# A decoder layer's first stage: a quarter of the value weighing on GpSimd, and context projections in token halves, one position at a time

## The chip, the cores and the metric

The kernel runs on one core of a Trainium2 chip. The metric is the device time of one execution in microseconds (us), the median of several runs. A core has a matrix engine (TensorE, PE in the profile), a vector engine (VectorE, DVE), an activation engine (ScalarE, ACT), GpSimd (POOL) and SyncE (SP), which here only issues DMA transfers. Each runs its own queue of instructions in order and waits on semaphores for the others. SBUF and PSUM are the memories on the chip, with 128 partitions each; TensorE writes its results to PSUM.

## The reference, cut to what matters

One post-norm decoder layer in float32 on `x` of 8 positions x 512 batch entries x 512 features, with a context of 8 x 512 tokens x 1024 features:

```python
q, k, v = split(x @ in_proj.T + bias)            # 16 heads of 32, sequence of 8
ac = einsum('tbhd,sbhd->bhts', q + r_w_bias, k)
bd = rel_shift(einsum('tbhd,rhd->bhtr', q + r_r_bias, p))
attn = softmax((ac + bd) * scale)
ctx = einsum('bhts,sbhd->tbhd', attn, v)
x = layernorm(x + ctx @ out_proj.T + b)
src = (context @ W_src.T + b_src) * mask         # 1024 -> keys 512, values 512
x = layernorm(x + cross_attention(x, src))       # 8 heads of 64, 512 tokens
x = layernorm(x + ffn(x))                        # 2048 hidden, second product in fp8
```

## The kernel before

The first stage does the self-attention and the first normalization; between those it projects the context to the keys and values that the second stage (cross-attention and feed-forward, the rest of the span) attends to.

**Self-attention.** Partitions are batch entries, four tiles j of 128. `keys`, `queries_of` and `values` project 128 x 512 tiles on TensorE through `project` (L225); keys and values go to `k_all`, `v_all` by ACT (L295 for values), queries to DVE (L254). The attention over eight positions is elementwise. For one query position t, `queries_of` forms on DVE, for two groups of eight heads, the product of the query with all keys (L258, 2048 elements a partition) and sums it over the head (L267). After eight positions `softmax` runs on the tile's scores `sc`: GpSimd adds offsets (L301), DVE subtracts the maximum and divides, ACT takes the exponential (L308). Then `weigh(j, t)` (L317 to L340) does, per position, for two groups of eight heads: a product of `v_all` with the broadcast weights (L322, 2048 elements), and three additions that halve the key positions (L332, L335, L338: 1024, 512 and 256 elements), the last into `ao`. `turn_out` transposes `ao` on TensorE (L346) two positions later, `put_out` projects it (L355), and the sum with `x` and the output bias (GpSimd, L365; DVE, L372), its statistics and normalization follow. `ao` has two buffers, `sc`, `k_all` and `v_all` have one.

**Context projections.** Seven products of block sums replace eight products of blocks (Winograd's form of Strassen's scheme). `halves(part)` loads the four blocks of the weight (keys are part 0, values part 1) and sums them (L141 to L144); `context_of(m, part)` loads the context of two positions, 2m and 2m + 1, as columns of one product, sums its blocks on DVE (`sums_of_b`, L148 to L151), and stores the sums to HBM (`td`), from where part 1 loads them again. `context_work` is a generator: for each part, for m = 0, 1, 2, for two halves i of the output rows, it issues seven products `py`, `pz`, `px`, `pz`, ... of four matmuls with 512 columns (L697), moves results by ACT (`put`, L727) and DVE (`add`, L739) to `kst` tiles, and stores them to `kd` or `vd` on ACT's queue. In between, `sum_w1` has GpSimd form sums of another weight, `w1`, for the second stage. Positions 0 to 5 are done so; position 6 is done with plain products of blocks (`project_context`, L171 for keys, L185 for values) at the end of the stage, position 7 in the second stage.

**The order of TensorE's work** is written out by a planner (L384 to L449, L810 to L875), with `manual_schedule` for PE; the other engines' instructions are ordered by the tile framework's scheduler. Each slot has a planned length: `SCORES` for a position of the scores, `SOFTMAX`, and `VALUES` for a position of the weighing. In a slot the planner places what must be there, then `spare` projections, and fills up with pieces of `context_work`. Each piece yields its cost (`FULL` = 3.54), `"between"` (something else must come first) or a negative number (rest for so long). SP's queue carries nearly all loads, the planner's order being that in which they are issued.

Of the kernel before, what the change touches and what calls it, by code (L numbers as in the profile page):

```python
# [42 lines left out]
def decoder_layer(  # L43
# [156 lines left out]
    with ExitStack() as ph:  # L200
# [116 lines left out]
        def weigh(j, t):  # L317
            ao[t] = qp.tile([P, E], F32, tag="ao", name=f"ao{j}_{t}")
            for g in range(2):
                fs = slice(g * HW, (g + 1) * HW)  # L320
                pr = prp.tile([P, T, HH, D1], F32, tag="pr", name=f"pv{j}_{t}_{g}")
                nc.vector.tensor_tensor(  # L322
                    pr,
                    v_all[j][:, :, fs].rearrange("p s (h d) -> p s h d", d=D1),
                    sc[j][:, t, g * HH * T : (g + 1) * HH * T]
                    .rearrange("p (h s) -> p s h", s=T)
                    .unsqueeze(3)
                    .to_broadcast([P, T, HH, D1]),
# [3 lines left out]
                nc.vector.tensor_tensor(  # L332
                    pf[:, 0:4, :], pf[:, 0:4, :], pf[:, 4:8, :], ALU.add
                )
                nc.vector.tensor_tensor(  # L335
                    pf[:, 0:2, :], pf[:, 0:2, :], pf[:, 2:4, :], ALU.add
                )
                nc.vector.tensor_tensor(  # L338
                    ao[t][:, fs], pf[:, 0, :], pf[:, 1, :], ALU.add
                )  # L340
# [43 lines left out]
        SCORES, SOFTMAX, VALUES, FULL = 11.2, 13.0, 12.4, 3.54  # L384
# [73 lines left out]
        with tc.tile_pool(name="setup", bufs=1) as sp:  # L458
# [140 lines left out]
        cxp = ph.enter_context(tc.tile_pool(name="cxp", bufs=8))  # L599
        tcp = ph.enter_context(tc.tile_pool(name="tcp", bufs=4))  # L600
        kst = ph.enter_context(tc.tile_pool(name="kst", bufs=4))
# [6 lines left out]
        PAIRS = 3  # L608
        td = [
            [dram.tile([P, 5, S], F32, name=f"td{m}_{f}") for f in range(HF)]  # L610
            for m in range(PAIRS)
        ]
# [12 lines left out]
        def context_of(m, part):  # L625
            lo, hi, tx = [], [], []
            for f in range(HF):
                a = cxp.tile([P, 2, S], F32, tag="ct", name=f"cl{part}{m}_{f}")
                b = cxp.tile([P, 2, S], F32, tag="ct", name=f"ch{part}{m}_{f}")
                x = tcp.tile([P, 3, S], F32, tag="tx", name=f"tx{part}{m}_{f}")  # L630

                def two(f):
                    return ctxT[2 * m : 2 * m + 2, f * P : (f + 1) * P, :].rearrange(
                        "t p s -> p t s"
                    )

                nc.sync.dma_start(b, two(HF + f))
                if part == 0:
                    nc.sync.dma_start(a, two(f))
                    with tc.high_priority():  # L640
                        sums_of_b(
                            nc.vector,
                            *(u[:, h] for u in (a, b) for h in (0, 1)),
                            *(x[:, i] for i in range(3)),
                        )
                    nc.sync.dma_start(td[m][f][:, 0:2], a)
                    nc.sync.dma_start(td[m][f][:, 2:5], x)
                else:
                    nc.sync.dma_start(a, td[m][f][:, 0:2])
                    nc.sync.dma_start(x, td[m][f][:, 2:5])  # L650
                lo.append(a)
                hi.append(b)
                tx.append(x)
            return lo, hi, tx
# [23 lines left out]
        def context_work():  # L678
            for part in range(2):
                store_w1()  # L680
                w7 = halves(part)
                blocks = [(4 * part + n, f) for n in range(4) for f in range(2)]
                if part:

                    yield -12.0
                for m in range(PAIRS):
                    lo, hi, tx = context_of(m, part)
                    b11, t3 = [u[:, 0] for u in lo], [u[:, 1] for u in lo]
                    b21, b22 = [u[:, 0] for u in hi], [u[:, 1] for u in hi]
                    t1, t2, t4 = ([u[:, i] for u in tx] for i in range(3))  # L690
                    for i in range(2):

                        def product(bank, a, b, start):


                            for f in range(HF):
                                nc.tensor.matmul(  # L697
                                    bank,
                                    lhsT=w7[:, a, f, i * P : (i + 1) * P],
                                    rhs=b[f],  # L700
                                    start=start and f == 0,
                                    stop=f == HF - 1,
                                    skip_group_check=not start,
                                )

                        def bank(name):
                            return ps_kv.tile(
                                [P, S], F32, tag="kv", name=f"{name}{part}{m}_{i}"
                            )

                        st = {}

                        def order(u, names):
                            if part == 0:
                                return u
                            return u.rearrange(f"p ({names}) -> p s g e", g=4, e=32)

# [15 lines left out]
                        def add(r, c, src):  # L736
                            dst = order(st[r, c], "g s e")
                            with tc.high_priority():
                                nc.vector.tensor_tensor(dst, order(src, "s g e"), dst, ALU.add)  # L739
# [43 lines left out]

        w6, ct6 = ([], []), []
# [1081 lines left out]
```

## Time and profile before

| | us |
|---|---|
| median of 3 runs (1992.72 to 1994.48) | 1994.43 |
| profiled execution | 1994.99 |
| its span, first to last instruction | 1993.2 |
| PE busy in the span | 1964.2 |
| DVE busy | 1580.8 |
| ACT busy | 563.9 |
| POOL busy | 246.7 |
| mean granted TensorE clock | 0.996 |
| first query projection of the second stage starts | 864.26 |

A group of the profile names line, engine, operation, output <- inputs by tile names, shape and count; then busy time in us and the mean of one in ns; then the engine's idle time just before them and what ended it. A float32 matmul stands as two rows, so counts of PE are twice the matmuls. The ends of matmuls are modelled; their distance from start to start is the surer measure. In a timeline, a line is a start, a length and a run of like instructions.

### The profile page before, as it was taken

To read this page: it belongs to the slowest core of one execution; us is meant where nothing else is said; L and a number is where in the kernel's file an instruction comes from. 1 tells how busy PE (TensorE), PEld (TensorE's weight loads), DVE (VectorE), ACT (ScalarE), POOL (GpSimd) and SP (SyncE) were. 2 spreads that over 40 slices of the span, in tenths; PEclk is the share of its full clock that TensorE was granted. 3 is DMA by queue.
4 is the path that set the end of the run, shared out by engine and by line. 5 is a ranking of instruction groups with operands and counts; after the bars stand their busy time and mean duration, and the time that the engine had idled before them with its cause. 6 is when DMAs were issued, how large, how long until landed. Compare 5 with 4: busy or idle time off the path is not lost.

```text
span 1993.2 us, 20470 instructions
## 1 busy us (share of the span) xinstructions
PE 1964.2 (99%) x6936; PEld 1108.3 (56%) x6936; DVE 1580.8 (79%) x2485; ACT 563.9 (28%) x1226; POOL 246.7 (12%) x264
## 2 busy tenths in 40 slices
PE   9999999998999999999999999999999999999998
PEld 4544444444444444443457657567576565676776
DVE  4999999899899989656885886877958868678443
ACT  2111111120111011123235244253352542535322
POOL 0030022002301121113401001002010010000000
PEclk9999999999999999999999999999999999999999
DMA  6635136252342361578698767775877767765721
GB/s 228 227 116 220 39 114 230 75 210 62 107 174 71 108 220 61 159 262 222 169 211 248 163 168 219 154 216 159 197 201 167 174 207 164 226 154 141 202 92 61
DMA packets 247080, 328.87 MB, mean 165 GB/s; under 512 B 85312, under 2 KB 140608, under 8 KB 242752
## 3 DMA queue, kind: packets, MB, share of 16 engines
q1 hardware_dynamic: 229200, 291.09, 52.0%
q10 hardware_dynamic: 14496, 25.47, 3.5%
q0 software_dynamic: 3280, 11.01, 1.8%
q8 instruction: 55, 0.90, 0.2%
q14 instruction: 49, 0.40, 0.1%
HBM read 195.90 MB, written 64.49 MB: 131 GB/s over the span
## 4 chain that ended last, share of the span: by engine, by line
PE 76%; DVE 19%; issue 2%; ACT 1%; DMA 1%; POOL 0%; SPq 0%; DVEq 0%; ACTq 0%
PE hx L1388 11%; PE s L1114 6%; PE pox L1306 6%; PE hz L1388 5%; PE av L1215 5%; PE psq L1093 5%; PE o L1480 5%; PE px L697 5%; DVE sc L267 4%; PE po L355 4%; DVE pq L258 4%; PE psk L171 3%; PE psv L185 3%; PE ps_q L225 3%; PE hy L1388 3%; PE poz L1306 3%
## 5 line engine op out<-in xcount | busy, mean ns | idle before, releaser
L1139 ACT ACTIVATE pe<-pe,nmax 128x512 f32<-128x512 f32 x256 | 182.8, 715 | 178.9 <-DVE nmax L1129 178.4
L1129 DVE CUSTOM_DVE_ANT_0 pe<-s,mb 128x512 f32<-128x512 f32 x256 | 162.8, 682 | 29.1 <-PE s L1114 25.4
L1162 DVE STREAM_TRANSPOSE pb<-pe 128x512 f32<-128x512 f32 x256 | 162.2, 681 | 5.4 <-DMA raw<-vd 2.8
L258 DVE TENSOR_TENSOR pq<-qw,k 128x2048 f32<-128x2048 f32 x64 | 152.5, 2383 | 1.2
L322 DVE TENSOR_TENSOR pv<-v,sc 128x2048 f32<-128x2048 f32 x64 | 146.9, 2295 | 6.5 <-ACT v L295 4.8
L267 DVE TENSOR_REDUCE sc<-pq 128x64 f32<-128x2048 f32 x64 | 145.9, 2280 | 1.0
L1114 PE MATMUL s<-kT,qTx 64*128 64x512 f32 x512 | 127.5, 616 | 0.5 <-DVE nmax L1129 0.5
L225 PE MATMUL ps_q<-w_in,xt 128*128 128x512 f32 x256 | 117.8, 604 | 5.2 <-DVE qw L254 5.2
L1215 PE MATMUL av<-pT,vx 128*64 128x512 f32 x512 | 118.6, 606 | 2.8 <-DMA raw<-vd 2.8
L1388 PE MATMUL hx<-x2s,w1r 128*128 128x256 f32 x512 | 119.5, 384 | 0.8 <-DVE hs L1416 0.8
L225 PE MATMUL ps_k<-w_in,xt 128*128 128x512 f32 x256 | 115.0, 601 | 4.5 <-DMA xt<-in_xT_dram 4.5
L1388 PE MATMUL hx<-x2T,w1r 128*128 128x256 f32 x512 | 118.4, 381 | 0.6 <-ACT hs L1410 0.6
L1154 DVE TENSOR_SCALAR pe<-pe,rden 128x512 f32<-128x512 f32 x256 | 115.3, 493 | 4.6
L355 PE MATMUL po<-w_o,aoT 128*128 128x512 f32 x256 | 115.3, 593 | 0.9 <-ACT aoT L371 0.9
L225 PE MATMUL ps_v<-w_in,xt 128*128 128x512 f32 x256 | 114.4, 593 | 0.1
L1480 PE MATMUL o<-w2q,hq 128*128 128x512 fp8e4 x512 | 114.4, 379 | 0.0
L1093 PE MATMUL psq<-x1Ts,w_tgt 128*128 128x512 f32 x256 | 113.8, 597 | 0.6 <-PE av L1215 0.6
L1388 PEld LDWEIGHTS hx<-x2s,w1r 128*128 128x128 f32 x512 | 95.5, 190 | 28.8 <-DVE nmax L1129 13.7
L1388 PEld LDWEIGHTS hx<-x2T,w1r 128*128 128x128 f32 x512 | 96.5, 190 | 20.5 <-issue 6.9
L1417 ACT ACTIVATE hq<-hs 128x512 fp8e4<-128x512 f32 x96 | 60.5, 630 | 144.7 <-DVE hs L1416 144.7
L697 PE MATMUL px<-tx,w 128*128 128x512 f32 x192 | 88.4, 604 | 3.6 <-DVE st L739 3.4
L365 POOL TENSOR_TENSOR r<-r,bo 128x512 f32<-128x512 f32 x32 | 48.9, 1545 | 330.0 <-DMA r<-in_x_dram 230.5
(204 smaller groups left out, 3066.0 us busy)
## 6 DMA issues: line engine op xcount, KB each, us to landing
pT<-pb SPq DMA_DIRECT2D x480, 128.0 KB, 2.4
w1r<-w1d SPq DMA_DIRECT2D x32, 1024.0 KB, 7.1
w1r<-w1d SPq DMA_DIRECT2D x32, 768.0 KB, 5.8
ch<-in_ctxT_dram SPq DMA_DIRECT2D x24, 512.0 KB, 5.7
td<-tx SPq DMA_DIRECT2D x12, 768.0 KB, 4.9
tx<-td SPq DMA_DIRECT2D x12, 768.0 KB, 7.5
r<-in_x_dram SPq DMA_DIRECT2D x32, 256.0 KB, 3.5
x1Ts<-x1d SPq DMA_DIRECT2D x32, 256.0 KB, 6.4
```

The lines of the kernel that those rows point to most:

```text
L225: nc.tensor.matmul(ps, lhsT=xt[:, e, :], rhs=w_in[:, e, part * E : (part + 1) * E], start=(e == 0), stop=(e == EC - 1),)
L258: nc.vector.tensor_tensor(pr, qw[:, fs] .rearrange("p (h d) -> p h d", d=D1) .unsqueeze(2) .to_broadcast([P, HH, T, D1]), k_all[j][:, :, f ...
L267: nc.vector.tensor_reduce(sc[j][:, t, g * HH * T : (g + 1) * HH * T], pr.rearrange("p h s d -> p (h s) d"), AX.X, ALU.add,)
L355: nc.tensor.matmul(po, lhsT=aoT[t][:, c * P : (c + 1) * P], rhs=w_o[:, c, :], start=(c == 0), stop=(c == EC - 1),)
L697: nc.tensor.matmul(bank, lhsT=w7[:, a, f, i * P : (i + 1) * P], rhs=b[f], start=start and f == 0, stop=f == HF - 1, skip_group_check=not s ...
L1093: nc.tensor.matmul(ps, lhsT=w_tgt[:, e, o * P : (o + 1) * P], rhs=x1T[t][:, e, :], start=(e == 0), stop=(e == EC - 1),)
L1114: nc.tensor.matmul(ps[:, h, :], lhsT=qT[t, c][half[h], j * P : (j + 1) * P], rhs=kT[t, c][half[h], :], start=True, stop=True,)
L1139: nc.scalar.activation(pe, pe, AF.Exp, bias=nmax[:, h : h + 1], scale=-1.0, accum_out=den[:, h : h + 1],)
L1215: nc.tensor.matmul(av[half[h], :], lhsT=v[t, c][:, s, half[h]], rhs=pT[t, c][:, :, :, s, h].rearrange("p g i q -> p (g i) q"), start=(s == 0),
L1306: nc.tensor.matmul(xo_bank[name][:, i], lhsT=b[:, e, i * P : (i + 1) * P], rhs=w[:, e], start=start and e + i == 0, stop=e == EC - 1, skip ...
L1388: nc.tensor.matmul(banks[g, name][:, i], lhsT=w[:, f, i * P : (i + 1) * P], rhs=b[:, f], start=start and f + i == 0, stop=f == 1, skip_gro ...
L1480: nc.tensor.matmul(po, lhsT=rows_of_j, rhs=w2q[:, c, :], start=(c == 0), stop=(c == HC - 1),)
```

## The change

In `weigh`, GpSimd takes heads 12 to 15 (with a buffer pool `pgp` of its own) and DVE heads 0 to 5 and 6 to 11, with the same four operations each, all writing parts of one `ao`. `SCORES` goes from 11.2 to 12.0, `VALUES` from 12.4 to 11.6.

The context projections take one position at a time: the columns of a product are one half of the position's 512 tokens, so a product is eight matmuls of 256 columns (four blocks of features, two halves h of the output rows, both in one PSUM bank) and not four of 512. Keys of positions 0 to 6 and values of positions 0 to 5 are done so; the plain keys of position 6 go. The blocks of a position (four raw, three sums, 512 KB each) are tiles of one pool of 13 (`cxp`), asked for in the order of use up to 13 products ahead. The rests of 13, 3 and 6 between positions are removed; that of 12 between the parts stays. Results of two row halves go to one `st` tile and are stored together.

The diff, cut to its core (the new `ask_blocks` and the new body of `context_work` in full, the lines that they replace being those of `context_of` and `context_work` above):

```diff
             ao[t] = qp.tile([P, E], F32, tag="ao", name=f"ao{j}_{t}")
-            for g in range(2):
-                fs = slice(g * HW, (g + 1) * HW)
-                pr = prp.tile([P, T, HH, D1], F32, tag="pr", name=f"pv{j}_{t}_{g}")
-                nc.vector.tensor_tensor(
+            for eng, lo, hi in (
+                (nc.gpsimd, 12, H1),
+                (nc.vector, 0, 6),
+                (nc.vector, 6, 12),
+            ):
+                hs = hi - lo
+                fs = slice(lo * D1, hi * D1)
+                pr = (pgp if eng is nc.gpsimd else prp).tile(
+                    [P, T, hs, D1], F32, tag="pr", name=f"pv{j}_{t}_{lo}"
+                )
+                eng.tensor_tensor(
                     pr,
                     v_all[j][:, :, fs].rearrange("p s (h d) -> p s h d", d=D1),
-                    sc[j][:, t, g * HH * T : (g + 1) * HH * T]
+                    sc[j][:, t, lo * T : hi * T]
                     .rearrange("p (h s) -> p s h", s=T)
                     .unsqueeze(3)
-                    .to_broadcast([P, T, HH, D1]),
+                    .to_broadcast([P, T, hs, D1]),
                     ALU.mult,
                 )
                 pf = pr.rearrange("p s h d -> p s (h d)")
-                nc.vector.tensor_tensor(
+                eng.tensor_tensor(
                     pf[:, 0:4, :], pf[:, 0:4, :], pf[:, 4:8, :], ALU.add
                 )
-                nc.vector.tensor_tensor(
+                eng.tensor_tensor(
                     pf[:, 0:2, :], pf[:, 0:2, :], pf[:, 2:4, :], ALU.add
                 )
-                nc.vector.tensor_tensor(
-                    ao[t][:, fs], pf[:, 0, :], pf[:, 1, :], ALU.add
-                )
+                eng.tensor_tensor(ao[t][:, fs], pf[:, 0, :], pf[:, 1, :], ALU.add)
...
-        SCORES, SOFTMAX, VALUES, FULL = 11.2, 13.0, 12.4, 3.54
+        SCORES, SOFTMAX, VALUES, FULL = 12.0, 13.0, 11.6, 3.54
...
-        cxp = ph.enter_context(tc.tile_pool(name="cxp", bufs=8))
-        tcp = ph.enter_context(tc.tile_pool(name="tcp", bufs=4))
-        kst = ph.enter_context(tc.tile_pool(name="kst", bufs=4))
+        BLOCKS = 13
+        pgp = ph.enter_context(tc.tile_pool(name="pgp", bufs=1))
+        cxp = ph.enter_context(tc.tile_pool(name="cxp", bufs=BLOCKS))
+        kst = ph.enter_context(tc.tile_pool(name="kst", bufs=2))
         HF, W2 = FC // 2, E // 2
-        PAIRS = 3
-        td = [
-            [dram.tile([P, 5, S], F32, name=f"td{m}_{f}") for f in range(HF)]
-            for m in range(PAIRS)
-        ]
+        KEYED, VALUED = T - 1, T - 2
+        td = [dram.tile([P, 5, HF, HALF], F32, name=f"td{m}") for m in range(VALUED)]
...
-        def context_of(m, part):
...
+        B21, T1, B11, T2, B22, T3, T4 = range(7)
+        KEPT = (T1, B11, T2, T3, T4)
+        parts = [(0, m) for m in range(KEYED)] + [(1, m) for m in range(VALUED)]
+        blocks_of, asked = {}, [0]
+        def ask_blocks(n):
+            for q in range(asked[0], min(n, 7 * len(parts))):
+                asked[0] = q + 1
+                part, m = parts[q // 7]
+                i = q % 7
+                b = blocks_of.setdefault((part, m), {})
+                b[i] = cxp.tile([P, HF, HALF], F32, tag="ct", name=f"ct{part}{m}_{i}")
+                raw = {B21: (1, 0), B22: (1, 1)}
                 if part == 0:
+                    raw |= {B11: (0, 0), T3: (0, 1)}
+                if i in raw:
+                    k, h = raw[i]
+                    src = chunked(ctxT[m])[
+                        :, k * HF : (k + 1) * HF, h * HALF : (h + 1) * HALF
+                    ]
+                    nc.sync.dma_start(b[i], src)
+                elif part:
+                    nc.sync.dma_start(b[i], td[m][:, KEPT.index(i)])
+                elif i == T4:
                     with tc.high_priority():
                         sums_of_b(
                             nc.vector,
+                            *(b[k] for k in (B11, T3, B21, B22, T1, T2, T4)),
                         )
+                    if m < VALUED:
+                        for k in KEPT:
+                            nc.sync.dma_start(td[m][:, KEPT.index(k)], b[k])
...
+            for n, (part, m) in enumerate(parts):
+                if m == 0:
+                    store_w1()
+                    w7 = halves(part)
+                    blocks = [(4 * part + g, f) for g in range(4) for f in range(2)]
+                    extra = len(blocks) - (VALUED if part else KEYED)
+                    if part:
+                        yield -12.0
+                def product(bank, a, i, start):
+                    ask_blocks(7 * n + i + BLOCKS)
+                    b = blocks_of[part, m][i]
+                    for f in range(HF):
+                        for h in range(2):
+                            nc.tensor.matmul(
+                                bank[:, h],
+                                lhsT=w7[:, a, f, h * P : (h + 1) * P],
+                                rhs=b[:, f],
+                                start=start and f + h == 0,
+                                stop=f == HF - 1,
+                                skip_group_check=not (start and h == 0),
+                            )
+                def bank(name):
+                    tl = ps_kv.tile([P, S], F32, tag="kv", name=f"{name}{part}{m}")
+                    return tl.rearrange("p (h q) -> p h q", h=2)
+                st = {}
+                def order(u, names):
+                    return u.rearrange(f"p ({names}) -> p s g e", g=4, e=32)
+                def target(r, c, h):
+                    if part == 0:
+                        return st[r][:, h, c * HALF : (c + 1) * HALF]
+                    return order(st[r][:, h], "g s e")[:, 2 * c : 2 * c + 2]
+                def put(r, c, src):
+                    if r not in st:
+                        st[r] = kst.tile([P, 2, S], F32, tag="st", name=f"st{part}{m}_{r}")
+                    with tc.high_priority():
+                        for h in range(2):
+                            if part == 0:
+                                nc.scalar.activation(
+                                    target(r, c, h),
+                                    src[:, h],
+                                    AF.Identity,
+                                    bias=col(C_BK + 2 * r + h),
+                                )
+                            else:
+                                nc.scalar.copy(
+                                    target(r, c, h), order(src[:, h], "s g e")
+                                )
+                def add(r, c, src):
+                    with tc.high_priority():
+                        if part == 0:
+                            y = st[r][:, :, c * HALF : (c + 1) * HALF]
+                            nc.vector.tensor_tensor(y, src, y, ALU.add)
+                        else:
+                            for h in range(2):
+                                y = target(r, c, h)
+                                nc.vector.tensor_tensor(
+                                    y, order(src[:, h], "s g e"), y, ALU.add
+                                )
+                def store(r):
+                    d = (kd, vd)[part][m]
+                    nc.scalar.dma_start(d[:, 2 * r : 2 * r + 2, :], st[r])
+                y = bank("py")
+                product(y, A12, B21, True)
+                yield FULL
+                put(0, 0, y)
+                z = bank("pz")
+                product(z, S1, T1, True)
                 store_w1()
+                yield FULL
+                put(1, 1, z)
+                x = bank("px")
+                product(x, A11, B11, True)
+                sum_w1(w7[:, 7], *blocks.pop(0))
+                yield FULL
+                add(0, 0, x)
+                yield "between"
+                product(x, S2, T2, False)
+                yield FULL
+                put(0, 1, x)
+                product(z, S4, B22, False)
+                store_w1()
+                yield FULL
+                add(0, 1, z)
+                store(0)
+                product(x, S3, T3, False)
+                if 0 < m <= extra:
+                    sum_w1(w7[:, 7], *blocks.pop(0))
+                yield FULL
+                add(1, 1, x)
+                yield "between"
+                product(x, A22, T4, False)
+                yield FULL
+                put(1, 0, x)
+                store(1)
...
-                        if i == 0 and m + part > 0:
-                            yield -6.0 if part else -13.0 if m == 1 else -3.0
...
-        def load_w6_keys():
-            w = kvp.tile([P, FC, E], F32, tag="k", name="w6k")
-            nc.sync.dma_start(w, chunked(w_srcT)[:, :, 0:E])
-            w6[0].extend(w[:, f, :] for f in range(FC))
-
         def load_w6_values():
-            for f in range(0, FC, 2):
-                w = cxp.tile([P, 2, E], F32, tag="ct", name=f"w6v{f}")
-                nc.sync.dma_start(w, chunked(w_srcT)[:, f : f + 2, E:])
-                w6[1].extend(w[:, i, :] for i in range(2))
+            w = kvp.tile([P, FC, E], F32, tag="k", name="w6v")
+            nc.sync.dma_start(w, chunked(w_srcT)[:, :, E:])
+            w6[1].extend(w[:, f, :] for f in range(FC))
...
-                if last and t == 0:
-                    spare += [(2 * FULL, piece) for piece in pieces[:EC]]
...
-        fill(clock + 2 * FULL)
```

## The prediction

> **What bounds the kernel now.** I read the page first, then busy time by stretches of the first stage, the waits of TensorE, its timeline, the groups of VectorE, and last the timelines of VectorE and GpSimd side by side.
>
> ```profile
> PE 1964.2 (99%) x6936; PEld 1108.3 (56%) x6936; DVE 1580.8 (79%) x2485; ACT 563.9 (28%) x1226; POOL 246.7 (12%) x264
> ```
>
> TensorE (PE) is busy 99% of the span. The change lies in the first stage, which ends when the next stage's first query projection starts, at 864.3 us. I cut it where VectorE (DVE) begins the scores of tiles j = 0, 1, 2 and 3 and where it writes its last `ao` (829 us):
>
> ```profile
> 42.00:250.00 208.00, 203.87 (x564) 97.26 (x564) 193.44 (x172) 31.17 (x61) 27.18 (x33) 0.99 0.41 146
> 250.00:452.00 202.00, 200.16 (x545) 94.17 (x544) 194.40 (x177) 31.34 (x51) 30.48 (x31) 1.00 0.46 158
> 452.00:637.00 185.00, 178.95 (x473) 83.63 (x472) 176.18 (x151) 27.02 (x45) 25.46 (x30) 0.98 0.29 97
> 637.00:829.00 192.00, 192.00 (x520) 90.53 (x519) 177.71 (x154) 27.39 (x45) 35.98 (x36) 1.00 0.38 130
> ```
>
> Columns: stretch, length, busy us of PE, weight load, DVE, ACT, POOL (GpSimd), clock. DVE is busy 193.4 + 194.4 + 176.2 + 177.7 = 742 of 787 us, so two engines are near full, and PE already waits for DVE:
>
> ```profile
> PE ps_q L225 <- DVE qw L254: 5.2, 1, 5.2
> ...
> PE px L697 <- DVE st L739: 3.4, 3, 2.3
> ...
> 488.01 6.17 PE L225 MATMUL ps_q<-w_in,xt 128*128 128x512 f32 x8 [5.22 <-DVE qw L254]
> 494.01 3.60 PE L225 MATMUL ps_v<-w_in,xt 128*128 128x512 f32 x8
> ```
>
> The first two are waits (total, times, longest); then, in the timeline, a projection after a wait takes 6.17 us instead of 3.60, so a wait also costs a slow restart. From matmul start to matmul start, TensorE loses some 21 us before 864 us to waits, loads and restarts.
>
> **The change, part by part.**
>
> *Weighing, what DVE gives up.* Per query position DVE now does two groups of six heads, not of eight.
>
> ```profile
> L322 DVE TENSOR_TENSOR pv<-v,sc 128x2048 f32<-128x2048 f32 x64 | 146.9, 2295 | 6.5 <-ACT v L295 4.8
> L332 DVE TENSOR_TENSOR pv<-pv 128x1024 f32<-128x1024 f32 x64 | 78.8, 1232 | 1.5
> L335 DVE TENSOR_TENSOR pv<-pv 128x512 f32<-128x512 f32 x64 | 45.3, 708 | 1.5
> L338 DVE TENSOR_TENSOR ao<-pv 128x256 f32<-128x256 f32 x64 | 28.3, 442 | 7.2 <-PE aot L346 5.0
> ```
>
> Undisturbed these take 2.29, 1.23, 0.69 and 0.43 us: 0.17 us plus 1.04 ns an element. So 1536, 768, 384 and 192 elements take 1.76, 0.96, 0.57 and 0.37 = 3.66 us, against 4.64: 0.98 us less, 64 times, is 63 us off DVE.
>
> *Weighing, what GpSimd takes on, and what that does to DVE.* GpSimd does 1024 + 512 + 256 + 128 = 1920 elements a position, all two-input operations out of SBUF. The timelines of DVE and of POOL at the same moment:
>
> ```profile
> 448.63 1.66 DVE L335 TENSOR_TENSOR pv<-pv 128x512 f32<-128x512 f32 x1
> 450.32 1.37 DVE L338 TENSOR_TENSOR ao<-pv 128x256 f32<-128x256 f32 x1
> 451.73 3.25 DVE L258 TENSOR_TENSOR pq<-qw,k 128x2048 f32<-128x2048 f32 x1
> ...
> 448.48 4.34 POOL L365 TENSOR_TENSOR r<-r,bo 128x512 f32<-128x512 f32 x3 [97.79 <-DMA r<-in_x_dram]
> 452.79 2.50 POOL L141 TENSOR_TENSOR w<-w 128x128 f32<-128x128 f32 x1
> ```
>
> Beside three GpSimd adds of 512 elements, three DVE operations take 1.66, 1.37 and 3.25 us, not 0.69, 0.43 and 2.29: +0.97, +0.94, +0.96. The last GpSimd operation, 0.45 us when alone, takes 2.50 because it waits for DVE's. They take turns, whole instruction by whole instruction: a GpSimd add of 512 costs DVE 0.96 us, 1.87 ns an element. Reductions do not suffer: the 19 of `sc<-pq` that ran mostly beside GpSimd took 2.28 us like the rest. Today's GpSimd work fits there, since the scores alternate product and reduction. The weighing does not: its eight DVE operations a position all read two SBUF operands, and GpSimd's share exists only then (it needs the softmax, and `sc` is wanted again for the next tile). So 1920 x 1.87 ns = 3.6 us a position, 115 us for 32, if each element meets such an operation. Below, the bound is nothing (all beside statistics and PSUM adds, a tenth of DVE's time in these phases). I take nine tenths, 105 us: the rows that look like this phase show full turns.
>
> The Trainium skill (SBUF — State Buffer, section "Who interferes with whom") states the same as a rule: a VectorE instruction with two SBUF inputs and a GpSimd instruction that reads SBUF lock each other out for a whole instruction. The trace agrees (+0.96 us). The same skill, GPSIMD Engine Reference, section "Engine selection", advises VectorE for elementwise work, GpSimd being about twice as slow on two inputs; by the row 512 elements take 1.27 us against 0.69. If that slowness were the only cost, GpSimd's time would lie beside DVE's and the 63 us would be a clear gain; by the lock rule it is a loss.
>
> *Context sums on DVE.* Before: 48 operations of 512 elements at 0.685 us = 33 us, and 36 additions from PSUM at 0.68 = 24.5. After: 28 sums of 1024 elements at 1.22 (row of `w<-w`) = 34, 21 additions at 0.68 for keys and 36 of 256 elements at about 0.43 for values = 30. DVE +7, taken as 8 for the strided ones.
>
> *TensorE.* Before, 12 x 7 = 84 products of 8 rows (a matmul of fp32 is two rows) and the direct keys of position 6 (32 matmuls). After, 91 products of 16 rows with 256 columns.
>
> ```profile
> 617.88 3.60 PE L697 MATMUL px<-cl,w 128*128 128x512 f32 x8
> 621.31 3.60 PE L355 MATMUL po<-w_o,aoT 128*128 128x512 f32 x8
> ...
> 1066.94 3.62 PE L1388 MATMUL hx<-x2T,w1r 128*128 128x256 f32 x16
> 1070.39 1.89 PE L1388 MATMUL hz<-x2s,w1r 128*128 128x256 f32 x8
> ```
>
> From start to start a product now takes 621.31 - 617.88 = 3.43 us; sixteen rows of 256 columns take 1070.39 - 1066.94 = 3.45, elsewhere in the second stage up to 3.56. Old: 84 x 3.43 + 8 x 3.43 = 316 us. New: 91 x 3.45 to 3.56 = 314 to 324. TensorE -2 to +8 us; I take +2.
>
> *Slots and rests.* SCORES + VALUES stay 23.6, so the plan's length stays; the rests of 13, 3 and 6 inside a part vanish because blocks roll in singly. That moves filler, it removes no matmul.
>
> *Queues.* SP issues 28 + 30 + 42 = 100 block transfers where it issued 84, of 512 KB, about the same bytes, and one load of `w6v` for five of `w6`. One block a product is 512 KB in 3.5 us at most, only where filler runs unbroken; a landing takes 5.7 us (`ch`) and thirteen blocks are a reach of nearly two positions: cost nothing. If that cover is gone, each late block costs its landing. ACT (122 us busy of 822) does 104 half-size copies for 48 and issues 26 stores for 48: nothing. On POOL the weighs share one queue with `r<-r,bo` and the `w1` sums.
>
> **The sum.** DVE work between 42 us and its last `ao`: 742 - 63 + 105 + 8 = 792. Of its 45 idle us I keep 30: 8.6 for the exponentials and 7.1 for GpSimd's offsets in the softmax are sure, the others shrink as DVE gets later. Last `ao`: 42 + 792 + 30 = 864 us, 35 later than now. TensorE now has 35 us of work behind that point; with DVE the later one it has only what needs it or stands behind it in the order: a turn (0.4), two output projections (6.9) and a value piece (6.9), 14 us. The next stage begins at 878, not 864: +14. The profiled execution has a span of 1993.2 and took 1995.0; 2007 + 1.8 = 2009 for it, and with its 0.5 above the median of the runs, **2008 us**.
>
> **Rivals.**
>
> *GpSimd's share costs DVE little: faster.* For: GpSimd is busy only 127 us from 42 to 864. The point: the last `ao` plus 14 us comes to 864 when the turns cost 742 + 8 - 63 + x + 30 = 808, x = 91 us, four fifths of the full 115. Below that TensorE bounds, and what DVE caused goes: waits of 5.2 + 3.4, and restarts of 6.17 - 3.60 and about 1.8 more, 13 us together, against TensorE's -2 to +8. That gives 1979 to 1989, say 1983. Against: the three rows show +0.96 each, with none hidden.
>
> *Near 91 us the two cancel*: 1990 to 1998.
>
> *GpSimd's order becomes the wait: slower still.* It runs its queue in order, and it now waits 230 us for the `r` loads and 188 us for `w1` loads, harmlessly. If a weigh stands behind such a wait, `aot` is late and TensorE stops for the landing, about 3.5 us, plus 2 for the restart. Eight of 32 are 44 us beside some of the forecast's 14: 2030 to 2050. For: longest waits of over 90 us. Against: `turn_out` comes two slots after the weigh.
>
> **How the numbers follow.** This kernel's measurement can tell about 0.2% (4 us) from no change. Forecast (turns cost over four fifths) 0.50, GpSimd's order 0.12: slower 0.62. Cancelling 0.13. Faster 0.25. The forecast's own bounds: all 115 us and idle kept at 45 give 42 + 847 + 14 = 903, +39, 2033; at x = 95 it is 1998. The range for eight in ten takes in most of the faster rival and part of the slowest: 1983 to 2038.
>
> **What would show it.** Right: the `pv` products on DVE average well over 1.76 us, the small ones double or more, values phases longer than today's 87 to 103 us, TensorE waiting at `ps_q` or `aot` for DVE, last `ao` near 864. Wrong: DVE's operations near their undisturbed lengths, or GpSimd's running beside the reductions after all. `py`, `px` and `pz` at 216 ns from row to row show the TensorE term right. Waits of `aot` on POOL would show the last rival; waits of `py` to `pz` on a DMA would show the rolling blocks late.

## The result, and the profile after

| | before | after |
|---|---|---|
| median of 4 runs, us | 1994.45 | 2072.82 (2066.84 to 2075.9) |
| ratio, 95% interval | | 1.0389, 1.0364 to 1.0414 |
| profiled execution, span | 1994.99, 1993.2 | 2066.84, 2065.0 |
| last `ao` | 828.7 | 907.8 |
| first query projection of the second stage | 864.3 | 938.4 |

The kernel is 3.9% slower: the forecast had the direction, but +78 us where it said +14, and 2073 lies above its range. Of the span's 71.8 us the first stage holds 74.1, so the second is 2 us shorter and holds none of the loss.

The line of the page that answers to the one of before:

```profile
PE 1979.3 (96%) x7656; PEld 1256.7 (61%) x7656; DVE 1625.0 (79%) x2486; ACT 569.5 (28%) x1278; POOL 458.2 (22%) x388
```

GpSimd is busy 211 us longer, VectorE 44, TensorE 15, in a span 72 us longer: TensorE now has room. The stretches, cut at the same points (columns as before):

```profile
42.00:274.00 232.00, 210.14 (x765) 139.30 (x765) 208.47 (x159) 33.15 (x77) 83.67 (x65) 0.96 0.47 157
274.00:484.00 210.00, 196.89 (x689) 124.61 (x688) 196.20 (x163) 31.91 (x61) 81.16 (x60) 0.98 0.31 101
484.00:692.00 208.00, 191.23 (x653) 119.85 (x652) 190.25 (x164) 29.25 (x58) 81.51 (x60) 0.96 0.37 115
692.00:908.00 216.00, 198.96 (x729) 133.38 (x728) 190.63 (x170) 28.83 (x61) 87.07 (x71) 0.96 0.36 115
```

VectorE's work is 785.6 us, forecast 792. But it is idle for 80.4 of these 866 us, against 45.0 of 786.7 before; the forecast had it falling to 30. TensorE now stands for part of every stretch, and its clock is below 1 in all four. The weighing on VectorE, groups from 42 to 908 us:

```profile
L329 DVE TENSOR_TENSOR pv<-v,sc 128x1536 f32<-128x1536 f32 x64 | 131.1, 2048 | 15.3 <-ACT v L295 13.6
L339 DVE TENSOR_TENSOR pv<-pv 128x768 f32<-128x768 f32 x64 | 92.9, 1451 | 1.7
L342 DVE TENSOR_TENSOR pv<-pv 128x384 f32<-128x384 f32 x64 | 58.0, 907 | 1.6
L345 DVE TENSOR_TENSOR ao<-pv 128x192 f32<-128x192 f32 x64 | 41.0, 640 | 5.2 <-PE aot L351 3.1
```

They take 2.05, 1.45, 0.91 and 0.64 us, and were to take 1.76, 0.96, 0.57 and 0.37 undisturbed. That is the exchange of turns, and one position shows it. VectorE's timeline first, then GpSimd's:

```profile
814.09 1.90 DVE L329 TENSOR_TENSOR pv<-v,sc 128x1536 f32<-128x1536 f32 x1
816.02 2.61 DVE L339 TENSOR_TENSOR pv<-pv 128x768 f32<-128x768 f32 x1
818.67 1.51 DVE L342 TENSOR_TENSOR pv<-pv 128x384 f32<-128x384 f32 x1
```

```profile
814.45 3.37 POOL L329 TENSOR_TENSOR pv<-v,sc 128x1024 f32<-128x1024 f32 x1
817.90 1.86 POOL L339 TENSOR_TENSOR pv<-pv 128x512 f32<-128x512 f32 x1
```

GpSimd's product (L329) ends at 817.82, and VectorE's sum of 768 elements, issued at 816.02, ends 0.81 us after that: it spent 1.8 of its 2.61 us waiting for GpSimd, which had itself waited for the VectorE instruction before (3.37 us for a product that takes it 1.96 at its shortest).

**Where the time is.** An engine's share over a whole stage hides this, so I cut each tile into its scores, its softmax (from the maximum, L304) and its values phase (the weighing, from the first `pv` to the last `ao`). The values phases of tiles 0 and 2, before and then after, by stretches:

```profile
147.00:249.70 102.70, 100.37 (x249) 45.30 (x248) 95.63 (x106) 17.88 (x29) 3.08 (x4) 0.98 0.35 130
...
550.40:637.10 86.70, 86.02 (x219) 39.10 (x218) 84.43 (x89) 14.86 (x25) 0.00 (x0) 1.00 0.32 119
```

```profile
155.30:274.10 118.80, 102.37 (x358) 68.02 (x357) 103.93 (x97) 18.84 (x38) 62.99 (x44) 0.94 0.37 124
...
587.60:692.20 104.60, 91.10 (x328) 62.47 (x327) 92.75 (x94) 15.19 (x32) 59.86 (x40) 0.93 0.36 112
```

Before, VectorE is busy for 84.4 of 86.7 us in such a phase: there is nothing to take an added microsecond. After, it is busy 8 us longer, but the phase is 18 longer, and TensorE's clock is 0.93 in it. Summed over the four tiles, from the same traces (TensorE "lost" is the distance from matmul start to matmul start, less what it is when nothing is in the way):

| us | scores | softmax | values | VectorE idle in values | TensorE lost in values |
|---|---|---|---|---|---|
| before | 420.8 | 38.2 | 369.7 | 15.2 | 8.1 |
| after | 427.0 | 49.2 | 431.6 | 42.7 | 76.3 |

The values phases hold 62 of the 79 us by which the last `ao` is later. (The softmax holds 11, of which 8.8 are one wait of VectorE for the values of the last tile, 13.6 us against 4.8. That wait is as long with the new projections and slots alone, so it is not GpSimd's.) TensorE's matmuls are the same work, 836.3 us against 837.5; its lost time in the stage rose from 22.3 to 97.2, which is the whole of the 74. What it waits for in the stage, the two largest entries of the list of waits (total, times, longest), and one such wait with its restart:

```profile
PE px L703 <- DVE st L747: 29.4, 5, 8.8
PE px L703 <- DVE st L751: 28.3, 6, 10.1
```

```profile
831.64 6.62 PE L703 MATMUL px<-ct,w 128*128 128x256 f32 x16 [10.07 <-DVE st L751]
838.10 3.62 PE L703 MATMUL pz<-ct,w 128*128 128x256 f32 x16
```

TensorE stands 10.07 us because the bank of `px` is still to be read by VectorE's addition into `st`, which stands in VectorE's queue among weighing operations; then sixteen rows take 6.62 us instead of 3.62. In the whole stage the granted clock is half for 64.9 us, of which TensorE works 40.9; before, it was 10.2 us and 8.4.

### The profile page after: what moved, and what is told of

Its sections match the earlier page's. It is cut to its first block, busy times and chain, and to the rows that moved or that the text cites. A ratio compares the mean times of both kernels' runs of the same rounds, so it can differ in the third digit from the quotient of the medians.

```text
span 2065.0 us, 22137 instructions
## 1 busy us (share of the span) xinstructions
PE 1979.3 (96%) x7656; PEld 1256.7 (61%) x7656; DVE 1625.0 (79%) x2486; ACT 569.5 (28%) x1278; POOL 458.2 (22%) x388
## 4 chain that ended last, share of the span: by engine, by line
PE 66%; DVE 26%; issue 4%; DMA 2%; ACT 1%; POOL 1%; SPq 0%; DVEq 0%; ACTq 0%; POOLq 0%
PE hx L1382 11%; PE s L1108 6%; PE pox L1300 5%; PE hz L1382 5%; PE av L1209 5%; PE o L1474 5%; PE psq L1087 5%; DVE pv L329 4%; DVE sc L267 3%; DVE pv L339 3%; PE px L703 3%; DVE pq L258 3%; PE poz L1300 3%; PE psv L185 3%; PE hy L1382 3%
## 5 line engine op out<-in xcount | busy, mean ns | idle before, releaser
L703 PE MATMUL px<-ct,w 128*128 128x256 f32 x832 | 207.8, 407 | 58.3 <-DVE st L747 29.4
L703 PEld LDWEIGHTS px<-ct,w 128*128 128x128 f32 x832 | 169.6, 206 | 101.8 <-DVE st L747 33.5
L329 DVE TENSOR_TENSOR pv<-v,sc 128x1536 f32<-128x1536 f32 x64 | 131.1, 2048 | 15.3 <-ACT v L295 13.6
L1065 POOL TENSOR_TENSOR vx<-vx,maskcol 128x512 f32<-128x512 f32 x24 | 24.9, 1039 | 525.1 <-DVE vx L1061 525.1
```

The costliest lines, as they stand in the source:

```text
L329: eng.tensor_tensor(pr, v_all[j][:, :, fs].rearrange("p s (h d) -> p s h d", d=D1), sc[j][:, t, lo * T : hi * T] .rearrange("p (h s) -> p ...
L703: nc.tensor.matmul(bank[:, h], lhsT=w7[:, a, f, h * P : (h + 1) * P], rhs=b[:, f], start=start and f + h == 0, stop=f == HF - 1, skip_grou ...
```

## The experiments

Theories: **A**, the turns that GpSimd and VectorE take on reads from SBUF lengthen the weighing, and that is the cost. **E**, what goes beyond that comes from waits that TensorE and VectorE impose on each other at the projections' PSUM banks. Other rivals (a mere reordering, GpSimd's queue, the projections or the slots by themselves) are described where an expectation uses them. "Before" stayed at 1994.4 to 1995.4 in all comparisons.

**1. The two halves of the change, each alone.** `rolling_alone` is the changed kernel with the old weighing and old slots:

```diff
-            for eng, lo, hi in (
-                (nc.gpsimd, 12, H1),
...
+            for g in range(2):
...
-        SCORES, SOFTMAX, VALUES, FULL = 12.0, 13.0, 11.6, 3.54
+        SCORES, SOFTMAX, VALUES, FULL = 11.2, 13.0, 12.4, 3.54
```

> The context projections of the change alone: VectorE weighs all 16 heads again, in two groups of eight, and the slots are those of before (11.2 and 12.4). Theory A (the lock between GpSimd and VectorE is the cause: it stretches the weighing, the additions that free the px bank stand behind it, TensorE stops and restarts at half clock): without the lock 1990 to 2005, VectorE's 8 us more for sums and little else; waits of px for st under 10 us. Rival B (the projections one position at a time are the cause: sums that wait for one of 13 tiles, more and smaller additions): 2040 or more, with the waits of px for st as after the change.

`weigh_alone` is the kernel before with the new weighing (for room `kst` has three buffers, not four, and `sma` one):

```diff
-            for g in range(2):
...
+            for eng, lo, hi in (
+                (nc.gpsimd, 12, H1),
+                (nc.vector, 0, 6),
+                (nc.vector, 6, 12),
+            ):
...
```

> GpSimd's four heads alone, on the kernel before with its projections in pairs and its slots; for room, kst has three tiles and not four and the small pool of the first stage one of each and not two. Theory A: 2040 to 2080, pv products of 1536 elements near 2.05 us and of 768 near 1.45 as after the change, TensorE waiting for VectorE's st. Rival B: at most 2010, since the pairs of positions with whole tiles leave more slack.

Measured: `rolling_alone` 2005.62, 1.0054 [1.0039, 1.0069], +10.5 us. `weigh_alone` 2039.66, 1.0216 [1.0199, 1.0233], +44. GpSimd's share carries most of the loss, and the projections cost by themselves. Apart the two make 55 us. Together, with the old slots too (`old_slots`, point 4), they make 64, so 9 us more than apart; the rest of the 78 comes with the new slots. In `rolling_alone` TensorE's waits at `px` for `st` are 17.0 us, where under 10 was expected. In `weigh_alone` VectorE's work rises by 32.0 us, but the last `ao` is 46.8 us later: more is lost than is added.

**2. Is it the turns?** `share_left_out` is the changed kernel without GpSimd's weighing:

```diff
+            nc.gpsimd.memset(ao[t][:, 12 * D1 :], 0.0)
...
-                (nc.gpsimd, 12, H1),
```

> The change, but the values of heads 12 to 15 are not weighed: GpSimd only writes zeros to their part of ao, which reads no SBUF; VectorE still does 12 heads. Theory A: the lock goes, pv products return to 1.76, 0.96, 0.56 and 0.36 us, and with 63 us less on VectorE the time falls below the kernel before, 1975 to 1990. Rival B: the stops stay, 2030 or more.

`writes_only` adds to that four fills of zeros per position on GpSimd, which read nothing:

```diff
+            pz4 = pgp.tile([P, T, 4, D1], F32, tag="pr", name=f"pv{j}_{t}_12")
+            for _ in range(4):
+                nc.gpsimd.memset(pz4, 0.0)
```

> The change, but heads 12 to 15 are not weighed: GpSimd instead writes zeros, four times over its product tile and once over its part of ao, so it is busy beside the weighing but reads no SBUF. Theory A (the lock on the shared read): 1990 to 2010, as without the share, VectorE's pv products at 1.76 us. Rival D (GpSimd's queue in order, or its mere being busy): 2035 or more.

`two_heads` gives GpSimd two heads, VectorE seven and seven:

```diff
-                (nc.gpsimd, 12, H1),
-                (nc.vector, 0, 6),
-                (nc.vector, 6, 12),
+                (nc.gpsimd, 14, H1),
+                (nc.vector, 0, 7),
+                (nc.vector, 7, 14),
```

> The change with GpSimd taking two of 16 heads instead of four (VectorE two groups of seven): half the elements on GpSimd, the same number of its instructions. Theory A with the price by elements: about half of the way from the projections alone (2006) to the change (2073), 2030 to 2045. Rival D (the number of hand-overs or the queue): 2055 or more.

Measured: `share_left_out` 1998.94, 1.0025 [1.0016, 1.0035]; `writes_only` 2015.62, 1.0098 [1.0083, 1.0113]; `two_heads` 2031.29, 1.0182 [1.0166, 1.0197]. VectorE's groups in `share_left_out`, the same operations on the same shapes with GpSimd quiet:

```profile
L329 DVE TENSOR_TENSOR pv<-v,sc 128x1536 f32<-128x1536 f32 x64 | 113.1, 1768 | 15.3 <-ACT v L295 13.6
L339 DVE TENSOR_TENSOR pv<-pv 128x768 f32<-128x768 f32 x64 | 62.9, 983 | 1.7
```

All four groups sum to 238.2 us here and to 323.0 in the changed kernel: the turns cost 85 us on these rows, and 92 on all of VectorE (785.4 against 693.4). Without the turns the time is 1999, not the 1975 to 1990 expected, since the projections and the slots cost 21 us by themselves (points 1 and 4).

In `writes_only` the fills wait for nobody, and GpSimd ran all 128 of them between 67.7 and 224.4 us, so that they lay beside the weighing of the first tile alone; the product's mean of 1774 ns says little, as 57 of the 64 products met no fill. VectorE's timeline and GpSimd's at a position that did meet fills:

```profile
181.81 1.76 DVE L332 TENSOR_TENSOR pv<-v,sc 128x1536 f32<-128x1536 f32 x1
183.61 0.96 DVE L342 TENSOR_TENSOR pv<-pv 128x768 f32<-128x768 f32 x1
184.60 0.56 DVE L345 TENSOR_TENSOR pv<-pv 128x384 f32<-128x384 f32 x1
```

```profile
179.93 5.99 POOL L321 MEMSET pv<- 128x1024 f32 x6
```

Beside fills the operations keep their undisturbed lengths, beside GpSimd's reads they do not: it is the reading that locks, not GpSimd's being busy. The 17 us of `writes_only` are another thing, as far as the waits show: in one place the fills stand ahead of the softmax offsets in GpSimd's queue, VectorE waits 18.1 us for these, and TensorE 18.5 for VectorE. No run keeps GpSimd busy with fills beside all of the weighing; but in the changed kernel's lists neither TensorE nor VectorE waits for GpSimd's weighing. So A holds. `two_heads` shows its limit: VectorE's work is 758.9 us, the same as with the new projections and slots alone (758.8, point 4), yet it is 15 us slower than these; TensorE's waits at `px` for `st` are 28.5 us there against 14.9. The sum of VectorE's work does not give the time.

**3. Are the mutual waits the excess?** `wider_gap` is the changed kernel with each pause between two uses of `px` doubled, so that more is placed between; `rolling_wider` the same on `rolling_alone`:

```diff
                 yield "between"
+                yield "between"
```

> The change with two other pieces, not one, between the addition that reads the px bank and TensorE's next product into it. Theory E (TensorE's stops at px, and the half clock after them, carry a large part of the loss beyond the lock's own time on VectorE): waits of px for st fall from 58 us to under 25, half clock from 65 us to under 35, 2025 to 2050. Rival F (VectorE is the bound and the stops only show it): the waits move to other products, 2063 or more.

> The projections alone (VectorE weighs 16 heads, slots of before) with the same wider gap. Theory E: the 17 us of waits of px for st go and with them most of the 11 us over the kernel before, 1992 to 2000. Rival F: 2003 or more.

`bank_by_act` lets ScalarE copy the product out of its bank, so that the bank no longer waits for VectorE (one copy buffer; `sma` has one, not two); `rolling_bank_by_act` is the same on `rolling_alone` (there `sma` keeps two):

```diff
+                        tmp = evp.tile([P, 2, HALF], F32, tag="ev", name=f"ev{part}{m}_{r}{c}")
+                        nc.scalar.copy(tmp, src)
+                        src = tmp
```

> The change, with ScalarE copying the px and pz banks to SBUF and VectorE adding from there, so that TensorE's next product waits for ScalarE alone (one tile for the copy; the small pool of the first stage has one buffer of each for room). Theory E (mutual waits at the px bank carry the loss beyond the lock): TensorE's waits of px for st, 58 us, go, half clock under 35 us, 2020 to 2045. Rival F (VectorE's lateness is met elsewhere): waits move to ps_q, aot or the copy, 2055 or more.

> The projections alone, VectorE weighing all heads, with the same copy by ScalarE. Theory E: the 17 us of waits of px go and with them the 10 us over the kernel before: 1992 to 1999. Rival F: 2002 or more.

Measured: `wider_gap` 2060.91, 1.0331 [1.0315, 1.0346], 12 us better than the changed kernel; `rolling_wider` 2016.96, 1.0110 [1.0093, 1.0126], 11 worse than its base; `bank_by_act` 2073.22, 1.0394 [1.0379, 1.0408], no gain; `rolling_bank_by_act` 1999.24, 1.0024 [1.0014, 1.0034], 6.4 better than its base. TensorE's waits in `bank_by_act`, then the one at `px` in `rolling_bank_by_act`:

```profile
PE px L704 <- ACT ev L747: 33.5, 5, 13.2
```

```profile
PE px L698 <- ACT ev L741: 1.2, 3, 0.7
```

With the old weighing the copy does what it is for: waits of 9.4 and 7.6 us at `px` become 1.2, although those for `qw` rise from 2.3 to 11.3. With GpSimd's share they mostly change their name, since the copy waits for a buffer that VectorE's addition has to free (ScalarE stands 37.0 us for that). In `wider_gap` the waits at `px` for `st` fall from 58 to 37 us, and the last `ao` comes 27 us earlier at the same work of VectorE (783 us); but 50 us of TensorE's work, not 31, is left after it. `wider_gap` lies between what E and F expected, `rolling_bank_by_act` at the upper end of E, the other two where F put them. So E is not the main cause, as these means take back at most 12 of the 78 us: the waits at `px` are where TensorE stops, not why. What makes the addition late is that VectorE is behind, and work taken from one place is missing in another. (With several copy buffers `bank_by_act` might differ; there was no room for them, and it was not tried.)

**4. The slots.** `old_slots` is the changed kernel with the old plan, `rolling_new_slots` is `rolling_alone` with the new one:

```diff
-        SCORES, SOFTMAX, VALUES, FULL = 12.0, 13.0, 11.6, 3.54
+        SCORES, SOFTMAX, VALUES, FULL = 11.2, 13.0, 12.4, 3.54
```

> The change with the slots of before, 11.2 for the scores and 12.4 for the values, so more filler is planned beside the weighing. Theory A: within 10 us of the changed kernel, 2063 to 2083, as the stops come from VectorE's lateness and not from where filler is planned. Rival C (the slots squeeze the filler into the wrong places): 2030 or less.

> The projections alone, VectorE weighing 16 heads, but with the change's slots, 12.0 and 11.6. If the slots by themselves cost what they cost the change (14 us): 2015 to 2025. If they only hurt where the lock makes the weighing long: 2000 to 2010.

Measured: `old_slots` 2059.28, 1.0322 [1.0305, 1.0339]; `rolling_new_slots` 2016.13, 1.0106 [1.0089, 1.0123]. The new slots cost 13.5 us with GpSimd's share, so that `old_slots` is faster than expected, and 10.5 without. They plan for weighing positions that are shorter than the old, and these are longer. From `rolling_new_slots` to the changed kernel, which differ in the weighing only, it is +56.7 us.

**5. The same share elsewhere.** `beside_reductions` is `share_left_out` with GpSimd doing nearly as many reads (29 positions of 32) during the scores, whose reductions do not lock:

```diff
+            if pgq:
...
+                nc.gpsimd.tensor_tensor(pg, kk, kk, ALU.mult)
+                nc.gpsimd.tensor_tensor(pf[:, 0:4, :], pf[:, 0:4, :], pf[:, 4:8, :], ALU.add)
...
```

> The change with heads 12 to 15 not weighed (GpSimd writes zeros to their part of ao), but with GpSimd doing the same four operations on as many elements in the scores, on squares of the keys that nobody uses, 29 times instead of 32. Same elements, same two-input reads of SBUF, but beside VectorE's reductions. Theory A (a turn costs only against a VectorE operation that reads two SBUF operands): most of GpSimd's time hides beside the reductions, VectorE's busy time rises by 20 to 45 us over the 693 without the share, and the time is 2000 to 2020. Rival G (GpSimd's reads cost VectorE the same wherever they stand): VectorE +90 us and 2045 or more.

Measured: 2059.08, 1.0321 [1.0307, 1.0335]. Inconclusive: GpSimd, which runs its queue in order, fell behind and came into the weighing all the same (`pv` 1887 ns, not 1768), VectorE's work rose by 62 us, and its fills of `ao` stood behind the added work, so that TensorE waited 22.6 us for them. It does show that this amount of reading did not fit beside the scores here.

**6. What would relief of VectorE be worth, and is there a better version?** `before_twelve` is the kernel before with the weighing of `share_left_out`. `act_normalize` is the kernel before with the normalization's last step on ScalarE. `before_bank` gives the kernel before the copy of point 3 (one buffer of `sma`), `before_bank_norm` both:

```diff
-                    normalize(rts[i], rts[i], mvs, rs, i)
+                    nc.scalar.activation(
+                        rts[i],
+                        rts[i],
+                        AF.Identity,
+                        bias=nb[:, i : i + 1],
+                        scale=rs[:, i : i + 1],
+                    )
```

> The kernel before, its projections in pairs and its slots, with heads 12 to 15 not weighed at all (zeros from GpSimd): what VectorE's 63 us would be worth if GpSimd's share were free. By the prediction's faster rival, up to 13 us of TensorE's stops go: 1980 to 1990. If TensorE's own order and loads keep the rest: 1991 to 1996.

> The kernel before with the first stage's 32 normalizations on ScalarE (scale and bias per partition) instead of VectorE, 15 us off VectorE for an engine that shares no port with it. If VectorE's time is worth about a third of itself, as 63 us would be by the faster rival at best: 1988 to 1993. If TensorE's stops stand elsewhere: within 2 us of before.

> The kernel before with ScalarE freeing the banks (one copy tile, one buffer each in the small pool). Its waits of px for st are 3.4 us with a restart of about 1.8: at best 1989 to 1993; if the additions from SBUF, now two-input ones that can meet GpSimd, cost as much: 1994 to 1998.

> The kernel before with both, banks freed and normalizations done by ScalarE: 1986 to 1992 if the two gains add, 1993 or more if TensorE's order keeps them.

Measured, in this order: `before_twelve` 1985.94, 0.9955 [0.9942, 0.9969]; `act_normalize` 1993.96, 0.9992 [0.9983, 1.0001]; `before_bank` 1999.19, 1.0019 [1.0010, 1.0028]; `before_bank_norm` 1994.04, 0.9995 [0.9987, 1.0004]. With a quarter of the weighing gone at no cost to anyone, 64 us less of VectorE's work, the old kernel gains 9 us, since TensorE's own 837.5 us of matmuls then fill nearly all of a stage of 855.6 us. None of the others beats the kernel before by an amount that can be told.

## Why the prediction was wrong in size

The steps, with what the runs measured:

| step | forecast | measured | by |
|---|---|---|---|
| weighing given up | −63 | −61 | `share_left_out`'s rows against before |
| turns on VectorE | +105 | +92 | changed kernel against `share_left_out` |
| context sums on VectorE | +8 | +12 | `ct` and `st` rows of `rolling_alone` (14 on all of VectorE); its 28 sums take 1.42 us, not 1.22 |
| VectorE's work to last `ao` | 792 | 785 | trace after |
| "of its 45 idle us I keep 30" | 30 | 80 | trace after |
| work of TensorE after it | 14 | 31 | trace after |
| TensorE's matmuls | +2 | −1 | trace after |
| slots | 0 | +10 to +14 | point 4 |
| queues | 0 | 0 to 3 | one wait of 3.3 us for a weight block |

The first three terms, all of which rested on rows, came out within 13 us each, and VectorE's work as a whole within 7. The 60 us that were missing in 938 (forecast 878) are the two terms in which work becomes time: idle +50, tail +17, work −7. **The step that failed is "of its 45 idle us I keep 30".** It treated the stage as one pool, in which 50 us more of VectorE's work could take up 15 us of idle time. By phases, 30 of those 45 us lay in the scores and the softmax, and the added work in the values phases, where VectorE was already busy for 354 of 370 us. There each turn lengthens the phase, and the lengthening is not confined to VectorE: TensorE finds its bank unread, stops, restarts at half speed, and then VectorE in its turn waits for TensorE, as the list of VectorE's waits in the changed kernel shows (nearly all in the values phases):

```profile
DVE st L747 <- PE px L703: 11.5, 2, 5.7
DVE st L751 <- PE px L703: 8.6, 2, 8.4
```

In the values phases VectorE waits 30.7 us for products and transposes of TensorE, against 8.2 in `rolling_new_slots`, which differs in the weighing only. Two engines that were both nearly full and hand work to each other did not take up each other's delays here; they added them. Of TensorE's 75 us of added lost time, standing makes about 59 and half speed 16 (an estimate: half of the 40.9 us worked at half speed, less half of the 8.4 before; no run took the restarts away alone). Not all of the 50 us between the forecast's 30 idle us and the measured 80 is the turns' doing. VectorE is idle for 56.0 us in `rolling_new_slots`, without GpSimd's share: 15 of the 50 are idle time that was never taken up, 11 came with the projections and slots, and 24 with the share.

The tail failed as well, but not by the turns, since it is 25 to 29 us in `rolling_alone`, `rolling_new_slots` and `share_left_out` too. The 14 us supposed that TensorE had done everything else by the last `ao`. It had not: three pieces of the values projection and three output projections came in these 30.6 us, where the forecast had one and two.

The term "slots and rests = 0" was wrong too. Moving filler removes no matmul, but it moves the places where one engine must wait for the other; +10.5 us with nothing else changed.

Of the rivals, the first put the point at which gain and loss cancel at about 91 us of turns. The turns were 92, and the first stage was still 74 us longer, so the point came from the same wrong conversion of work into time. Its price, about 1983 where VectorE's relief is free, is near `before_twelve`'s 1985.94. GpSimd's queue order, the slow rival, is not it: the changed kernel has a single wait of TensorE on `ao`, 0.4 us and for VectorE's part. The signs named beforehand did show: `pv` well over 1.76 us, values phases of 101 to 119 us, `py` to `pz` at 216 ns a row; but TensorE stopped mostly at `px` (57.7 us for `st`), hardly at `ps_q` (0.7) or `aot` (4.2).

What stays open: `two_heads` is 15 us slower than `rolling_new_slots` at equal work of VectorE, and no run separates longer single operations from their changed order there. That the parts add up (projections 10.5, slots 10.5, GpSimd's share 57) holds in this order only: on the old projections the share costs 44.

## What to carry to other kernels

Work out added work phase by phase, between the points where one engine's results are due, and count as free only the idle time inside the phase that gets it. Where two engines near full wait for each other, add to the work the stops that it causes, and look for the buffer at which the one stands until the other has read it. Moving work to a second engine relieves the first only where the two do not lock each other out of memory, as they did here; see from one timeline of both engines whether they run side by side or in turns.

## What the runs showed of the hardware

- Turns cost VectorE 85 us on the 256 weighing operations, for 61,440 elements a partition that GpSimd read in pairs: 1.38 ns an element where a full exchange costs 1.87. GpSimd is held up as well: its product takes 2.64 us on average, 1.96 at its shortest.
- Fills of 1024 elements on GpSimd (0.95 us each) leave VectorE's two-input product at 1.76 us and its sum of 768 elements at 0.96, as with GpSimd quiet (`share_left_out`, 1768 and 983 ns on average). The Trainium skill (SBUF — State Buffer, section "Who interferes with whom") says that a GpSimd instruction that only writes does not contend with such a product; these figures agree.
- Short stops are followed by half speed too: in the kernel before, a wait of 2.33 us at 171.82 us is followed by eight rows in 5.40 us instead of 3.60, with the granted clock at half for 3.4 us. The Trainium skill (TensorE: Matmul & The Clock Gate, "Part 1: The HAM clock gate (the "warmup" mystery)") gives at least one idle window of about 3.4 us as what it takes, the windows running freely; here TensorE stood for only 2.33 us, and the measurement decides.
